# Four graph layers in one kernel: a longer lag between two streams of work, and plain f32 in place of split fp32r matmuls

## The chip, the cores and the metric

The kernel runs on one core of one Trainium2 chip. The metric is the time of one execution on the device in microseconds. The profile is one execution of the same program. In it PE is TensorE (PEld its weight loads), DVE is VectorE, ACT is ScalarE, POOL is GpSimd, and SP issues the transfers of inputs and outputs.

## What is computed

The input is 64 graphs of 256 nodes with 256 features, and a 0/1 adjacency matrix for each. Four layers follow each other; every one takes `h = relu(layernorm(x))` and adds its result to `x`.

```
# layer 0: attention with 4 heads of 64
Wh = h @ W;  e = leaky_relu(e_src[i] + e_dst[j], 0.2), masked by adj
x += elu(softmax(e) @ Wh)
# layer 1: attention with 4 heads and 5 edge types
w = sum over t of (adj == t+1) * (e_src[t, i] + e_dst[t, j])
w = leaky_relu(w, 0.01), masked where adj == 0
o = relu(softmax(w) @ Wh + bias) + Wh
x += layernorm(o, per head) * gamma + beta
# layer 2: attention with one head of 256
x += softmax(masked leaky_relu(src[i] + dst[j], 0.2)) @ Wh
# layer 3: three rounds of a gated graph unit on h
for i in range(3):
    aggr = A.T @ (h @ weight[i])        # A = (adj != 0)
    h = gru_cell(aggr, h, w_ih, w_hh, b_ih, b_hh)
x += h
```

## The kernel before

Two graphs are handled together, so there are NP = 32 pairs. A pair is 512 rows, in C = 4 blocks of 128 partitions. Two Python generators write out the work of a pair. `attention(xt, at)` (line 320) writes layers 0, 1 and 2; `gru(p, xt, at)` (line 438) writes layer 3. Each `yield` ends a step: attention has NA = 50 steps and the GRU NB = 32 (lines 538 and 539).

`together` (line 526) interleaves the steps of attention of pair p with those of the GRU of pair p - 1, in the proportion NA to NB, and it ends only when both are done (lines 541 to 548). So there are 33 slots: one with attention alone, 31 with both, one with the GRU alone. `load(p + 1)` is written at the start of slot p. Tiles come from pools with a fixed number of buffers: `loads` 3, `work` 2 unless said otherwise, `small` 3, and two pools of 4 PSUM banks each, `psa` for attention (and for the norm of the GRU) and `psb` for the rest of the GRU. The order of issue on each engine is made from the written order by a scheduler; it may move an instruction ahead of others when its operands and a buffer are there. Each engine then works through its own queue.

The steps of attention, as far as they matter here:

- `norm_t` (line 188) takes statistics of a row on DVE (193, 194), makes the inverse deviation on POOL (196, 197), normalises on DVE (200), transposes on PE (208) and applies the relu on ACT (211). For the GRU it also returns the rows themselves.
- `project` (line 228) multiplies by the layer's weights (233); ACT brings the result to SBUF (237).
- A head of layer 0 makes its scores (258, then 340 on DVE with the mask `cap0`), then `softmax_t` (275 and 277 on DVE, 280 on ACT, transposes 290 on PE, copies 297 on DVE and 299 on ACT), then `attend_head` (305 on PE, 314 on DVE).
- A head of layer 1 does five score broadcasts (258), one for each edge type. ACT adds the source score while it brings one to SBUF (377), and DVE copies it under the mask of that type (381). Softmax and attend follow as in layer 0.
- The end of layer 1 is a normalisation per head, on DVE, POOL and ACT in turn (387 to 407). Layer 2 has one head (267, 418, 432).

The broadcast of a row of destination scores to all partitions is a matmul. `dst_rows` (line 240) makes all rows of a layer by one accumulated matmul in f32 (244) and splits them into a high half in type fp32r (249) and the remainder (250), which lie on two groups of 32 partitions. `dst_row` (line 255) then multiplies them by a 0/1 column of `sel` in one fp32r matmul, whose sum over partitions puts the two halves together.

A round of the GRU aggregates over the graph (451), applies twelve gates, each a matmul group of 512 columns (467), with ACT, DVE and POOL work between them (478 to 495), and transposes the new state back to rows (508). The adjacency `am` (441) is 0/1. It is held in fp32r, and the rows are split into `hh` and `hl` (215 and 216 for the first round, 520 and 521 for the others), so the aggregation takes four fp32r matmuls where two f32 ones would be written. In the last round the rows are added to `x` (514, tile `y`, in the buffers of `xn`) and sent out (523).

Of the kernel before, what the change touches and what calls it, by code (L numbers as in the profile page):

```python
# [8 lines left out]
F32 = mybir.dt.float32  # L9
I32 = mybir.dt.int32  # L10
U8 = mybir.dt.uint8
F32R = mybir.dt.float32r
AF = mybir.ActivationFunctionType
OP = mybir.AluOpType
# [9 lines left out]
def kernel(  # L24
# [24 lines left out]


    nc = tc.nc
    B, N, D = x.shape
    H, T, E = a1_src.shape
    L = w3t.shape[0]
    P = 128
    DC = D // P
    C = 2 * N // P
    S = 2 * N
# [14 lines left out]
    w2e = consts.tile([P, DC, D + 1], F32, name="w2e")  # L73

    Q = 32
    w0d = consts.tile([P, DC, 2 * Q], F32, name="w0d")
    w1d = consts.tile([P, DC, 2 * Q], F32, name="w1d")
    nc.vector.memset(w0d, 0.0)
    nc.vector.memset(w1d, 0.0)

    sel = consts.tile([2 * Q, Q], F32R, name="sel")
    nc.vector.tensor_add(sel, ident[: 2 * Q, :Q], ident[: 2 * Q, Q : 2 * Q])
    w2d = consts.tile([P, DC, 1], F32, name="w2d")
# [19 lines left out]
    with tc.tile_pool(name="setup", bufs=1) as sp, tc.tile_pool(  # L103
# [19 lines left out]
        for dc in range(DC):  # L123
            for s, (d0, d1, d2) in enumerate(
                (
                    (w0e[:, dc, D:], w1e[:, dc, D:], w2e[:, dc, D:]),
                    (w0d[:, dc, :H], w1d[:, dc, :HT], w2d[:, dc, :]),
                )
# [12 lines left out]
                nc.vector.tensor_reduce(d2, tmp.rearrange("p h e -> p (h e)"), AX.X, OP.add)  # L141

        for dc in range(DC):
            nc.vector.tensor_copy(w0d[:, dc, Q : Q + H], w0d[:, dc, :H])
            nc.vector.tensor_copy(w1d[:, dc, Q : Q + HT], w1d[:, dc, :HT])

# [20 lines left out]

    loads = ctx.enter_context(tc.tile_pool(name="loads", bufs=3))
    work = ctx.enter_context(tc.tile_pool(name="work", bufs=2))
# [8 lines left out]
    def bank(pool):  # L178
        return pool.tile([P, S], F32, name="bank_" + pool.name, tag="bank_" + pool.name)
# [8 lines left out]
    def norm_t(xt, want_rows=False):  # L188
# [23 lines left out]
        if not want_rows:  # L212
            return ht
        hh, hl = halves()
        nc.vector.tensor_scalar(hh, xn, 0.0, None, op0=OP.max)
        nc.vector.scalar_tensor_tensor(
            hl, xn, 0.0, hh.bitcast(F32), op0=OP.max, op1=OP.subtract
        )
        return ht, (hh, hl)

    def halves():

        return (
            work.tile([P, C, D], F32R, name="hh"),
            work.tile([P, C, D], F32R, name="hl"),
        )

    def project(ht, we, m):
# [9 lines left out]
        return wh  # L238

    def dst_rows(ht, wd):  # L240

        ps = bank(psa)
        for dc in range(DC):
            nc.tensor.matmul(  # L244
                ps[: 2 * Q, :], lhsT=wd[:, dc, :], rhs=ht[:, dc, :],
                start=(dc == 0), stop=(dc == DC - 1),
            )
        ed = work.tile([2 * Q, S], F32R, name="ed")
        nc.scalar.copy(ed, ps[: 2 * Q, :])
        nc.vector.tensor_tensor(  # L250
            ed[Q:, :], ps[Q : 2 * Q, :], ed[Q:, :].bitcast(F32), op=OP.subtract
        )
        return ed

    def dst_row(ed, r):

        ps = bank(psa)
        nc.tensor.matmul(  # L258
            ps, lhsT=sel[:, r : r + 1].to_broadcast([2 * Q, P]), rhs=ed, start=True, stop=True
        )  # L260
        return ps

# [57 lines left out]
    def attention(xt, at):  # L320
# [10 lines left out]
        wh = project(ht, w0e, D + H)  # L331
        ed = dst_rows(ht, w0d)
        yield
        o = work.tile([P, C, D], F32, name="o")
        for h in range(H):
            ps = dst_row(ed, h)
            u = work.tile([P, C, N], F32, name="u", bufs=3)
            for c in range(C):
                b = c // 2
                nc.vector.scalar_tensor_tensor(  # L340
                    u[:, c, :], ps[:, b * N : (b + 1) * N], wh[:, c, D + h : D + h + 1],
                    cap0[:, c, :], op0=OP.add, op1=OP.min,
                )
            yield
            pt, rs = softmax_t(u, 0.2)
            yield
            attend_head(o, pt, rs, wh, h)
            yield
# [15 lines left out]
        wh = project(ht, w1e, D + HT)  # L364
        ed = dst_rows(ht, w1d)
        yield
        o = work.tile([P, C, D], F32, name="o")
        for h in range(H):
            u = work.tile([P, C, N], F32, name="u", bufs=3)
            nc.gpsimd.tensor_copy(u, base)  # L370
            for t in range(T):
                r = t * H + h
                ps = dst_row(ed, r)
                e = work.tile([P, C, N], F32, name="e")
# [63 lines left out]
    def gru(p, xt, at):  # L438

        am = work.tile([P, C, N], F32R, name="am", bufs=1)  # L440
        nc.vector.tensor_scalar(am, at, 0.0, None, op0=OP.not_equal)
        ht, hn = norm_t(xt, want_rows=True)
        yield
        for i in range(L):
            ag = work.tile([P, DC, S], F32, name="ag")
            for dc in range(DC):
                ps = bank(psb)
                for b in range(2):
                    for k in range(4):
                        part, c = hn[k % 2], 2 * b + k // 2  # L450
                        nc.tensor.matmul(  # L451
                            ps[:, b * N : (b + 1) * N],
                            lhsT=part[:, c, dc * P : (dc + 1) * P],
                            rhs=am[:, c, :],
                            start=(k == 0), stop=(k == 3),
                        )
                nc.scalar.copy(ag[:, dc, :], ps)
# [40 lines left out]
            last = i == L - 1  # L498
            if last:
                y = work.tile([P, C, D], F32, name="y", tag="xn")  # L500
            else:
                hn = halves()
            for b in range(2):
                ps = bank(psb)
                for ic in range(2):
                    for dc in range(DC):
# [4 lines left out]
                            ident,  # L511
                        )
                if last:
                    nc.vector.tensor_add(
                        y[:, 2 * b : 2 * b + 2, :].rearrange("p c d -> p (c d)"),
                        xt[:, 2 * b : 2 * b + 2, :].rearrange("p c d -> p (c d)"), ps,
                    )
                else:
                    hh, hl = (v[:, 2 * b : 2 * b + 2, :].rearrange("p c d -> p (c d)") for v in hn)
                    nc.scalar.copy(hh, ps)  # L520
                    nc.vector.tensor_tensor(hl, ps, hh.bitcast(F32), op=OP.subtract)
            yield
        nc.sync.dma_start(out_v[:, p * C : (p + 1) * C, :], y)
        yield

    def together(a, na, b, nb):

        done_a = done_b = 0
        ended = object()
        while a is not None or b is not None:  # L530
            if b is None or (a is not None and done_a * nb <= done_b * na):
                a = None if next(a, ended) is ended else a
                done_a += 1
            else:
                b = None if next(b, ended) is ended else b
                done_b += 1

    NA = 2 + 3 * H + 1 + H * (T + 2) + 3 + 4
    NB = 2 + L * (2 + 4 * DC)
    tiles = {0: load(0)}  # L540
    for p in range(NP + 1):
        if p + 1 < NP:
            tiles[p + 1] = load(p + 1)
        together(
            attention(*tiles[p]) if p < NP else None, NA,
            gru(p - 1, *tiles[p - 1]) if p else None, NB,
        )
        tiles.pop(p - 1, None)

# [37 lines left out]
```

## Time and profile before

Every number is in microseconds unless it says otherwise.

| what | value |
|---|---|
| time, median of 3 runs | 6597.33 (6597.02 to 6597.98) |
| time of the profiled execution | 6597.33 |
| its span, first to last instruction | 6595.5 |
| mean granted clock of TensorE | 0.80 of full |
| PE busy | 4860.4 (74%), 17584 records |
| weight loads busy | 2973.5 (45%) |
| DVE busy | 3744.0 (57%) |
| ACT busy | 2796.1 (42%) |
| POOL busy | 1445.3 (22%) |
| gates, line 467, PE | 1208.9 + 1151.3 |
| score broadcasts, line 258, PE | 336.0, 768 records |
| aggregation, line 451, PE | 269.4 + 269.8, 1536 records |
| eviction of layer 1 scores, line 377, ACT | 969.7 |
| masked copies of layer 1, line 381, DVE | 853.1 |
| bytes moved | 59.05 MB, mean 9 GB/s |

A busy PE is not a PE at its peak, since matmuls are pipelined and their ends are modelled. The granted clock is the share of full speed that TensorE's clock had. The time of the profiled execution is 1.8 over the span: what lies around the span is small and fixed. Where a view gives an idle time and an arrow, the instruction after the arrow is the one that ended the wait.

### The profile page before, as it was taken

To read this page: it belongs to the slowest core of one execution; us is meant where nothing else is said; L and a number is where in the kernel's file an instruction comes from. 1 tells how busy PE (TensorE), PEld (TensorE's weight loads), DVE (VectorE), ACT (ScalarE), POOL (GpSimd) and SP (SyncE) were. 2 spreads that over 40 slices of the span, in tenths; PEclk is the share of its full clock that TensorE was granted. 3 is DMA by queue.
4 is the path that set the end of the run, shared out by engine and by line. 5 is a ranking of instruction groups with operands and counts; after the bars stand their busy time and mean duration, and the time that the engine had idled before them with its cause. 6 is when DMAs were issued, how large, how long until landed. Compare 5 with 4: busy or idle time off the path is not lost.

```text
span 6595.5 us, 52281 instructions
## 1 busy us (share of the span) xinstructions
PE 4860.4 (74%) x17584; PEld 2973.5 (45%) x17584; DVE 3744.0 (57%) x5955; ACT 2796.1 (42%) x7021; POOL 1445.3 (22%) x935
## 2 busy tenths in 40 slices
PE   4676877777877768777778777687777787776877
PEld 2444544444544444444445444444444454444443
DVE  4555655655555556555555556565555555565653
ACT  2344443444533444434445334444344443344442
POOL 1222122221222221222212222212222122222121
PEclk6777888777878778887778787788877787877888
DMA  1000000000000000000000000000000000000000
GB/s 55 0 10 10 4 10 7 10 10 4 10 7 10 10 10 4 10 7 10 10 4 10 7 10 10 10 4 10 7 10 10 4 10 7 10 10 7 0 4 7
DMA packets 55356, 59.05 MB, mean 9 GB/s; under 512 B 3120, under 2 KB 54192, under 8 KB 55088
## 3 DMA queue, kind: packets, MB, share of 16 engines
q1 hardware_dynamic: 54080, 53.88, 2.7%
q8 instruction: 139, 2.28, 0.1%
q10 hardware_dynamic: 1008, 1.84, 0.1%
q14 instruction: 129, 1.06, 0.1%
HBM read 38.93 MB, written 16.78 MB: 8 GB/s over the span
## 4 chain that ended last, share of the span: by engine, by line
PE 57%; DVE 17%; ACT 13%; POOL 9%; issue 4%; DMA 0%; DVEq 0%; ACTq 0%; SPq 0%; POOLq 0%
PE bank_psb L467 23%; PE bank_psa L305 10%; ACT e L377 9%; PE bank_psa L233 6%; PE bank_psb L451 4%; PE bank_psa L290 4%; PE bank_psa L258 3%; PE bank_psa L208 2%; DVE u L275 2%; PE bank_psa L244 2%; POOL var L402 1%; POOL en L351 1%; DVE nm L277 1%; POOL d L493 1%; POOL o L405 1%
## 5 line engine op out<-in xcount | busy, mean ns | idle before, releaser
L467 PE MATMUL bank_psb<-ht,whh 128*128 128x512 f32 x2304 | 1208.9, 637 | 0.0
L467 PE MATMUL bank_psb<-ag,wc 128*128 128x512 f32 x2304 | 1151.3, 604 | 0.0
L377 ACT ACTIVATE e<-bank_psa,wh 128x256 f32<-128x256 f32 x2560 | 969.7, 481 | 175.7 <-PE bank_psa L258 174.6
L493 POOL TENSOR_TENSOR d<-ht,n 128x512 f32<-128x512 f32 x192 | 273.1, 1422 | 3329.0 <-ACT n L487 3329.0
L381 DVE COPY_PREDICATED u<-masks,e 128x1024 f32<-128x1024 uint8 x640 | 853.1, 1333 | 255.1 <-ACT e L377 247.6
L208 PE MATMUL bank_psa<-ident,xn 128*128 128x128 f32 x1024 | 205.4, 352 | 909.4 <-DVE xn L200 889.9
L280 ACT ACTIVATE u<-u,nm 128x256 f32<-128x256 f32 x1152 | 571.1, 497 | 619.0 <-DVE nm L277 619.0
L305 PEld LDWEIGHTS bank_psa<-wh,pt 128*128 128x128 f32 x4608 | 738.9, 233 | 124.4 <-issue 61.0
L305 PE MATMUL bank_psa<-wh,pt 128*128 128x64 f32 (+1 forms) x4608 | 788.8, 332 | 1.8
L290 PE MATMUL bank_psa<-ident,u 128*128 128x128 f32 x2304 | 480.3, 333 | 375.5 <-ACT u L280 373.8
L467 PEld LDWEIGHTS bank_psb<-ht,whh 128*128 128x128 f32 x2304 | 445.7, 206 | 445.6 <-issue 433.3
L290 PEld LDWEIGHTS bank_psa<-ident,u 128*128 128x128 f32 x2304 | 334.0, 167 | 677.8 <-ACT u L280 580.9
L208 PEld LDWEIGHTS bank_psa<-ident,xn 128*128 128x128 f32 x1024 | 155.2, 177 | 1018.2 <-issue 857.1
L467 PEld LDWEIGHTS bank_psb<-ag,wc 128*128 128x128 f32 x2304 | 402.4, 191 | 405.6 <-issue 405.0
L211 ACT ACTIVATE ht<-bank_psa 128x512 f32<-128x512 f32 x256 | 142.6, 595 | 942.5 <-PE bank_psa L208 939.0
L314 DVE TENSOR_TENSOR o<-bank_psa,rs 128x256 f32<-128x256 f32 x256 | 108.3, 423 | 535.8 <-PE bank_psa L305 535.8
L297 DVE COPY pt<-bank_psa 128x512 f32<-128x512 f32 x288 | 197.9, 687 | 330.6 <-PE bank_psa L290 326.3
L451 PE MATMUL bank_psb<-am,hh 128*128 128x256 f32 x768 | 269.4, 379 | 154.4 <-ACT hh L520 153.3
L508 PE MATMUL bank_psb<-ident,ht 128*128 128x128 f32 x768 | 195.7, 388 | 232.1 <-DVE ht L495 212.6
L275 DVE SCALAR_TENSOR_TENSOR u<-u 128x1024 f32<-128x1024 f32 x288 | 351.1, 1219 | 3.5
L277 DVE TENSOR_REDUCE nm<-u 128x4 f32<-128x1024 f32 x288 | 349.6, 1214 | 3.5
L258 PE MATMUL bank_psa<-ed,sel 64*128 64x512 f32 x768 | 336.0, 509 | 5.0 <-DVE ed L250 2.8
(98 smaller groups left out, 6541.7 us busy)
## 6 DMA issues: line engine op xcount, KB each, us to landing
xt<-in_x_dram SPq DMA_DIRECT2D x32, 512.0 KB, 4.7
at<-in_adj_dram SPq DMA_DIRECT2D x32, 512.0 KB, 3.8
out_dram<-y SPq DMA_DIRECT2D x32, 512.0 KB, 3.2
whh<-in_L_gnn_w_hh_dram SPq DMA_DIRECT2D x1, 768.0 KB, 10.1
w<-in_L_gnn_weight_dram SPq DMA_DIRECT2D x3, 256.0 KB, 3.0
wih<-in_L_gnn_w_ih_dram SPq DMA_DIRECT2D x1, 768.0 KB, 5.9
a1b<-in_L_gnn_a_src_dram ACTq DMA_DIRECT2D x1, 640.0 KB, 7.2
a1b<-in_L_gnn_a_dst_dram ACTq DMA_DIRECT2D x1, 640.0 KB, 10.2
```

Source lines behind the costliest of these rows:

```text
L208: nc.tensor.transpose(ps[:, c * P : (c + 1) * P], xn[:, c, dc * P : (dc + 1) * P], ident)
L233: nc.tensor.matmul(ps[:, :m], lhsT=ht[:, dc, c * P : (c + 1) * P], rhs=we[:, dc, :m], start=(dc == 0), stop=(dc == DC - 1),)
L258: nc.tensor.matmul(ps, lhsT=sel[:, r : r + 1].to_broadcast([2 * Q, P]), rhs=ed, start=True, stop=True)
L275: nc.vector.scalar_tensor_tensor(u, u, slope, u, op0=OP.mult, op1=OP.max)
L277: nc.vector.tensor_reduce(nm, u, AX.X, OP.max, negate=True)
L280: nc.scalar.activation(u[:, c, :], u[:, c, :], AF.Exp, bias=nm[:, c : c + 1], accum_out=sm[:, c : c + 1])
L290: nc.tensor.transpose(ps[:, jc * N + ic * P : jc * N + (ic + 1) * P], u[:, 2 * b + ic, jc * P : (jc + 1) * P], ident,)
L305: nc.tensor.matmul(ps, lhsT=pt[:, b, jc, ic * P : (ic + 1) * P], rhs=wh[:, 2 * b + jc, f0:f1], start=(jc == 0), stop=(jc == 1),)
L377: nc.scalar.activation(e[:, c, :], ps[:, b * N : (b + 1) * N], AF.Identity, bias=wh[:, c, D + r : D + r + 1],)
L381: nc.vector.copy_predicated(u, masks[:, t], e)
L451: nc.tensor.matmul(ps[:, b * N : (b + 1) * N], lhsT=part[:, c, dc * P : (dc + 1) * P], rhs=am[:, c, :], start=(k == 0), stop=(k == 3),)
L467: nc.tensor.matmul(ps, lhsT=w[:, dc, g * P : (g + 1) * P], rhs=v[:, dc, :], start=(k == 0), stop=(k == n - 1),)
```

## The change

Two things are changed together.

The first is the type of the matmuls with a 0/1 operand. All are plain f32 now. In layer 0 `dst_rows` is gone: each head computes and broadcasts its scores in one step with `dst_scores`, a function that layer 2 already used, with two accumulated matmuls of full depth. In layer 1 the rows are still made once (without the padding to 64) and copied once by ACT; each broadcast is one f32 matmul with a column of `ident`. In the GRU, `am` and the rows `hn` are f32, the aggregation takes two f32 matmuls instead of four fp32r ones, the relu of the first rows is one POOL instruction, and the later rows are brought back by one copy on DVE and one on ACT.

The second is the order of writing. The loop of slots is gone. One generator runs the attention of all pairs, another the GRU of all pairs. The GRU starts one and a half passes of attention later (`lag = NA + NA // 2`), and both then advance in the proportion NA to NB without a stop at the end of a pair. `loads` has four buffers in place of three, and the last rows take a buffer of `hn` in place of one of `xn`.

```diff
-    loads = ctx.enter_context(tc.tile_pool(name="loads", bufs=3))
+    loads = ctx.enter_context(tc.tile_pool(name="loads", bufs=4))
...
-        hh, hl = halves()
-        nc.vector.tensor_scalar(hh, xn, 0.0, None, op0=OP.max)
-        nc.vector.scalar_tensor_tensor(
-            hl, xn, 0.0, hh.bitcast(F32), op0=OP.max, op1=OP.subtract
-        )
-        return ht, (hh, hl)
+        hn = work.tile([P, C, D], F32, name="hn")
+        nc.gpsimd.tensor_scalar(hn, xn, 0.0, None, op0=OP.max)
+        return ht, hn
...
         ht = norm_t(xt)
         wh = project(ht, w0e, D + H)
-        ed = dst_rows(ht, w0d)
         yield
...
-            ps = dst_row(ed, h)
+            ps = dst_scores(ht, w0d, h)
...
-        ed = dst_rows(ht, w1d)
+        ps = bank(psa)
+        for dc in range(DC):
+            nc.tensor.matmul(
+                ps[:HT, :], lhsT=w1d[:, dc, :], rhs=ht[:, dc, :],
+                start=(dc == 0), stop=(dc == DC - 1),
+            )
+        ed = work.tile([HT, S], F32, name="ed", bufs=1)
+        nc.scalar.copy(ed, ps[:HT, :])
...
-                ps = dst_row(ed, r)
+                ps = bank(psa)
+                nc.tensor.matmul(
+                    ps, lhsT=ident[:HT, r : r + 1].to_broadcast([HT, P]), rhs=ed,
+                    start=True, stop=True,
+                )
...
-        am = work.tile([P, C, N], F32R, name="am", bufs=1)
+        am = work.tile([P, C, N], F32, name="am", bufs=1)
...
-                    for k in range(4):
-                        part, c = hn[k % 2], 2 * b + k // 2
+                    for sc in range(2):
                         nc.tensor.matmul(
                             ps[:, b * N : (b + 1) * N],
-                            lhsT=part[:, c, dc * P : (dc + 1) * P],
-                            rhs=am[:, c, :],
-                            start=(k == 0), stop=(k == 3),
+                            lhsT=hn[:, 2 * b + sc, dc * P : (dc + 1) * P],
+                            rhs=am[:, 2 * b + sc, :],
+                            start=(sc == 0), stop=(sc == 1),
                         )
...
-            if last:
-                y = work.tile([P, C, D], F32, name="y", tag="xn")
-            else:
-                hn = halves()
+            hn = work.tile([P, C, D], F32, name="hn")
...
+                elif b == 0:
+                    nc.vector.tensor_copy(dst, ps)
                 else:
-                    hh, hl = (v[:, 2 * b : 2 * b + 2, :].rearrange("p c d -> p (c d)") for v in hn)
-                    nc.scalar.copy(hh, ps)
-                    nc.vector.tensor_tensor(hl, ps, hh.bitcast(F32), op=OP.subtract)
+                    nc.scalar.copy(dst, ps)
...
-    tiles = {0: load(0)}
-    for p in range(NP + 1):
-        if p + 1 < NP:
-            tiles[p + 1] = load(p + 1)
-        together(
-            attention(*tiles[p]) if p < NP else None, NA,
-            gru(p - 1, *tiles[p - 1]) if p else None, NB,
-        )
-        tiles.pop(p - 1, None)
+    tiles = {}
+
+    def attentions():
+        for p in range(NP):
+            if p not in tiles:
+                tiles[p] = load(p)
+            if p + 1 < NP:
+                tiles[p + 1] = load(p + 1)
+            yield from attention(*tiles[p])
+
+    def grus():
+        for p in range(NP):
+            yield from gru(p, *tiles.pop(p))
...
+    lag = NA + NA // 2
+    a, b = attentions(), grus()
+    for k in range(NA * NP + lag):
+        next(a, None)
+        if k >= lag:
+            for _ in range((k - lag + 1) * NB // NA - (k - lag) * NB // NA):
+                next(b, None)
+    for _ in b:
+        pass
```

## The prediction

> **What bounds the kernel now.** I first asked how regular the run is. Line 388 runs once per pair; the answer for that line gives its first and last start, and so does that of line 208 for the first transposes of pair 0 and of the last GRU.
>
> ```profile
> L388 DVE SCALAR_TENSOR_TENSOR o<-o,wh x32: 1224/1226/1227, 216.7 to 6459.8; 128x1024 f32<-128x1024 f32 x32
> L208 PE MATMUL bank_psa<-ident,xn x1024: 272/328/477, 59.8 to 6507.7; 128*128 128x128 f32 x171
> ```
>
> (6459.8 - 216.7) / 31 = 201.4 us per pair. The span is 59.8 (set-up and first load) + 32 x 201.4 + about 92 for the last pair's GRU alone (its inputs are final at 6503, the span ends at 6595.5): 6596. So the question is the 201.4.
>
> I cut one steady pair at three marks: A, layer 0 (from the end of one attention to line 354), B, layer 1 up to line 388, C, the normalisation of layer 1 and layer 2. Below it are the same stretches of pair 0, where no GRU runs. Columns: length, then busy time of PE, PEld, DVE, ACT, POOL, then the granted clock.
>
> ```profile
> core 0: us, PE busy (x) PEld busy (x) DVE busy (x) ACT busy (x) POOL busy (x), PEclk, DMA share, GB/s
> 665.40:722.80 57.40, 55.31 (x232) 33.61 (x231) 33.30 (x55) 24.76 (x60) 9.47 (x7) 0.94 0.00 0
> 722.80:822.40 99.60, 76.31 (x253) 44.40 (x251) 61.13 (x79) 54.84 (x141) 14.15 (x9) 0.80 0.02 6
> 822.40:865.00 42.60, 17.51 (x60) 12.71 (x60) 20.89 (x49) 6.85 (x17) 20.85 (x12) 0.62 0.08 25
> ...
> 60.00:123.00 63.00, 35.71 (x128) 26.50 (x127) 25.15 (x42) 14.97 (x44) 7.17 (x5) 0.55 0.03 9
> 123.00:218.00 95.00, 42.14 (x144) 30.00 (x144) 49.67 (x61) 44.20 (x123) 8.29 (x5) 0.55 0.00 0
> 218.00:260.00 42.00, 17.04 (x55) 12.39 (x56) 18.88 (x44) 6.41 (x16) 20.86 (x12) 0.61 0.00 0
> ```
>
> The reader should see two things. A pair takes 200 us with or without its GRU: attention is a chain that no engine fills. And the GRU is not free: alone the chain runs at half clock, with the GRU at 0.94, and what the clock gives, the GRU's matmuls take. A is full (55.3 of 57.4), C is empty, because the GRU ended in B. The list of waits has that hole, and the chain of waits has the GRU's matmuls (467) ahead of attention's work:
>
> ```profile
> PE bank_psa L208 <- DVE xn L200: 889.9, 66, 24.4
> ...
> PE bank_psb L467 23%; PE bank_psa L305 10%; ACT e L377 9%; PE bank_psa L233 6%; PE bank_psb L451 4%; PE bank_psa L290 4%; PE bank_psa L258 3%; PE bank_psa L208 2%; DVE u L275 2%; PE bank_psa L244 2%; POOL var L402 1%; POOL en L351 1%; DVE nm L277 1%; POOL d L493 1%; POOL o L405 1%
> ```
>
> Next, what keeps the order. This is the timeline of pair 0 at the change from one head to the next:
>
> ```profile
> 79.17 3.68 PE L305 MATMUL bank_psa<-wh,pt 128*128 128x64 f32 x16
> ...
> 82.77 0.79 PE L258 MATMUL bank_psa<-ed,sel 64*128 64x512 f32 x1
> 82.88 0.42 DVE L314 TENSOR_TENSOR o<-bank_psa,rs 128x256 f32<-128x256 f32 x1 [3.69 <-PE bank_psa L305]
> 83.60 1.66 DVE L340 SCALAR_TENSOR_TENSOR u<-bank_psa,wh,cap 128x256 f32<-128x256 f32 x4 [0.30 <-PE bank_psa L258]
> ```
>
> The score of the next head needs only ed, ready 11 us before, and PE was idle in between; still it comes after line 305. Work that takes banks of pool psa keeps the written order. Other work doesn't: line 441, written for a GRU of the next slot, runs at 61.4. GRU matmuls take banks of psb and run ahead of their written place, but its norm_t takes psa.
>
> **What the Trainium skill says.** "TensorE: Matmul & The Clock Gate", Part 1, gives 1.2 GHz after an idle window of about 3.4 us and 2.4 GHz after a busy one; the trace agrees (0.50 where PE idles in C, 1.00 in dense GRU work). The same page, "Architectural detail", has ACT and DVE as strict FIFO and PE pulling only weight loads ahead; the matmuls of this trace agree, and so a score behind a GRU group waits for it. No page prices the fp32r type; the trace does.
>
> **The price of a matmul**, at clock 1.00, from the starts in the timeline:
>
> ```profile
> 384.45 1.88 PE L467 MATMUL bank_psb<-ht,whh 128*128 128x512 f32 x4
> 386.16 1.88 PE L467 MATMUL bank_psb<-ag,wc 128*128 128x512 f32 x4
> ...
> 380.26 0.72 PE L258 MATMUL bank_psa<-ed,sel 64*128 64x512 f32 x2
> ...
> 671.66 0.28 PE L451 MATMUL bank_psb<-am,hh 128*128 128x256 f32 x1
> 671.78 0.28 PE L451 MATMUL bank_psb<-am,hl 128*128 128x256 f32 x1
> ```
>
> An f32 matmul appears as two records: four records in 1.71, so 0.43 each and 0.86 for one matmul of 512 columns. The fp32r score is one record: two in 0.72 against 0.50 for one alone, so 0.22. The aggregation's records of 256 columns start 0.12 apart; in f32 I take half of 0.43, 0.215.
>
> **The change part by part**, per pair.
>
> PE work. Layer 1 scores: 20 x (0.86 - 0.22) = +12.8. Layer 0 scores, now two full-depth f32 matmuls per head: 4 x (1.72 - 0.22) = +6.0; its dst_rows goes: -1.7. Aggregation: 16 f32 records in place of 16 fp32r in each of 3 GRU layers: 48 x (0.215 - 0.12) = +4.6. Sum +21.7 us on 149 busy, 694 us over the run. What reaches the chain:
>
> Stage A. For heads 1 to 3 the score stands between line 305 and line 340: 1.5 later, less the 0.2 by which line 314 covers it: +3.9. Head 0 loses the cast and subtraction of ed: in the steady pair line 244 ends at 669.5 and line 340 starts at 671.55; -2. Net +2. At half clock a score costs 3.4 in place of 0.8 (+2.6 each, +6 net); if PE warms up during it, +2.
>
> Stage B. The first score of each head is exposed: 4 x 0.64 = 2.6; less line 250 (0.7): +1.9. The other 16 scores run under ACT's four evictions (969.7 us / 640 = 1.5 per score). In the half with GRU work, some 10 scores take 6.4 us of PE that is 80% busy: I charge half, +3. In the half without it, at half clock, a score lasts 1.7, over the 1.5 of ACT: +2. Sum +7; bounds +2 (all hidden) and +15 (all of the 12.8 and the 2).
>
> GRU. Aggregation +4.6, half charged: +2. Off DVE: lines 250 (1.4), 215 and 216 (1.9) and four of 0.68 for line 521, against two copies of 0.69: -4.6; off ACT two copies of 0.6 and a cast; half of it lay on the chain of GRU or attention at most: I take -1. POOL gains one relu over 1024 elements, 2.8 as on line 351; POOL is 22% busy, so it delays only the first aggregation of a pair, while attention runs: 0; uncovered, 2.8.
>
> The new order. GRU's norm_t uses psa, xn and the statistics tiles, so by the rule above it stands at its written place: one and a half passes after its attention began, inside head 1 of layer 1 of the next pair. From there it will run about 140 us as now (669 to 808): some 50 of B, all of C, some 45 of the next A. Then nothing is ready for it until the next midpoint. So the hole of PE moves from C to late A and early B, of some 60 us, rather than vanish. C: PE pieces at full clock (projection 5.5 to 3.8, transposes 2.1 to 1.0 and 2.4 to 1.0, line 305 5.1 to 3.5) save 5.7; against it stand five matmul groups of the chain, each behind half a GRU group on average (0.9), and GRU's lines 483, 486, 494, 495 (0.69 each) and 493 (1.3 on POOL, whose next chain operation then waits for ACT's line 487): about +6. Net 0. A and B lose a third of the GRU work: contention there is 57.4 against some 48 (63 alone, at full clock for its 35.7 of PE), and about 10 in B, so 20 x 1/3 = -7; and the 60 us of half clock cost +5 (63 alone against 57.4 in A is 5.6 for such a stretch). Net -2.
>
> Loads get a fourth buffer: at 9 GB/s mean and a load a pair ahead, 0. Its SP queue holds loads and outputs only.
>
> Sum: 2 + 7 + 2 - 1 + 0 - 2 = +8, less 2 because the norm_t of the GRU, now behind a started head, leaves the start of A: T = 201.4 + 6 = 207.5.
>
> Ends. Attention starts at 60 as before. When it ends, GRU 30, begun some 100 us earlier, has about 30 us left, and GRU 31 needs 92 + 3 for the f32 aggregation, 125 in all in place of 92. Time: 60 + 32 x 207.5 + 125 = 6825 us. The profiled execution took 6597.33, which is the median of the three runs, 1.8 over the span; I make no difference between the two.
>
> **The rivals.**
>
> 1. Faster. The GRU's matmuls spread evenly, PE stays warm throughout, and the relief outweighs the price: A falls to 50 + 2, B to 95 + 5, C to 42: T = 194, 60 + 6208 + 125 = 6393. For it: the chain has 27% GRU matmuls on it, and C's hole of 24 us is large. Against it: f32 hands back 21.7 of PE, and GRU work runs ahead of its written place whenever PE is free, so it bunches. It decides below T = (6595 - 185) / 32 = 200.3: the half pair of longer lag at the end costs 33 us, so a pair must gain 1.1 us before anything is won.
>
> 2. Slower by much: the GRU's waits enter the chain of C. POOL, DVE and ACT serve seven dependent steps there, and each queue holds them behind GRU instructions that wait for each other; at 1.5 us more for each of ten crossings C gets 15 longer, and with B's upper bound, A's +6: T = 216 to 220, up to 7200. For it: in the steady pair PE sits idle at 749 to 754 behind line 508.
>
> 3. No difference: T = 199.9 to 200.7.
>
> 4. The change doesn't do what it says, the order of issue still running the GRU as early as now. Then C stays empty and A and B pay all the f32: T near 217, about 7130. The pool order speaks against it; I count it with rival 2.
>
> **How the numbers follow.** Likeliest, T from 203 to 213 (6680 to 7000): 0.52. Rival 1 with its neighbours: 0.19. Rivals 2 and 4: 0.24. Same within 0.2%, which is about what a measurement of this kernel can tell from no change: 0.05. Slower 0.76. The range of 6480 to 7080 leaves out the better half of rival 1 and the worse part of rival 2, about 0.2.
>
> **What would show it.** Right: line 388 recurs every 207 us; C has PE busy above 30 us; line 208's wait of 889.9 is mostly gone; PE clock of late A near 0.6; no GRU matmul in some 60 us before its norm_t; PE busy up by 600 or more; the last GRU work begins about 125 before the end. Wrong: A under 53, or a clock above 0.9 in all stages (rival 1); C above 52 (rival 2); PE idle in C (rival 4). The least certain term is how much of the GRU's work delays attention.

## The result, and the profile after

The changed kernel takes 6754.74 us (median of 4, 6748.02 to 6759.49), the kernel before 6597.18 on the same chip. The ratio is 1.0238, 95% interval 1.022 to 1.0256: slower. 6825 was predicted, with a range of 6480 to 7080. The profiled execution took 6748.02, 1.8 over its span.

The lines have moved. Line 388 of before is now 354, 208 is 197, 467 is 432, 258 is 336 in layer 1 and 223 in layers 0 and 2, 377 is 343, 381 is 347, 432 is 398, 451 is 416, and 493, 494 and 495 are 458, 459 and 460.

The answers for two lines, with the first and the last start of each:

```profile
L354 DVE SCALAR_TENSOR_TENSOR o<-o,wh x32: 1224/1226/1227, 228.3 to 6583.7; 128x1024 f32<-128x1024 f32 x32
L197 PE MATMUL bank_psa<-ident,xn x1024: 272/421/478, 59.7 to 6653.8; 128*128 128x128 f32 x171
```

A pair takes (6583.7 - 228.3) / 31 = 205.0 in place of 201.4. This time from one pair to the next is called the period below. The 150.7 by which the span grew divides into 11.6 before the first of these marks (228.3 against 216.7), 31 x 3.62 = 112.3 between them, and 26.8 after the last (162.5 against 135.7).

A steady pair, cut at the same marks into A, B and C. Columns: length, busy time of PE, PEld, DVE, ACT and POOL, then the granted clock:

```profile
core 0: us, PE busy (x) PEld busy (x) DVE busy (x) ACT busy (x) POOL busy (x), PEclk, DMA share, GB/s
3150.30:3206.60 56.30, 48.00 (x205) 29.25 (x203) 31.86 (x51) 19.86 (x52) 8.86 (x6) 0.97 0.10 28
3206.60:3308.10 101.50, 88.87 (x261) 49.87 (x262) 57.27 (x79) 52.82 (x137) 15.27 (x10) 0.76 0.00 0
3308.10:3355.20 47.10, 35.50 (x114) 20.04 (x113) 25.51 (x49) 13.18 (x27) 23.98 (x14) 0.93 0.00 1
```

With its marks set as exactly, the kernel before has A 60.6, B 98.3, C 42.5 (the prediction's A of 57.4 began 1.8 late and ended 1.5 early, which adds 1.5 to its B). C is full of GRU work now, and warm, which means that PE's clock is granted near full (0.93; cold is half clock), and it is 4.6 longer. A is shorter by 4.3, B longer by 3.2. The sum of PE is 172.4; before it was 150.6 in these marks.

The list of waits and the chain of waits:

```profile
DVE u L347 <- ACT e L343: 634.8, 573, 12.0
PE bank_psa L197 <- DVE xn L189: 634.0, 66, 24.2
ACT e L343 <- PE bank_psa L336: 425.4, 252, 5.0
```

```profile
PE bank_psb L432 15%; PE bank_psa L336 11%; PE bank_psa L261 8%; PE bank_psa L212 6%; PE bank_psa L246 5%; PE bank_psa L223 4%; ACT e L343 4%; PE bank_psb L416 3%; DVE nm L233 2%; DVE u L347 2%; POOL cap L281 2%; ACT u L236 2%; PE bank_psa L197 2%; DVE u L295 2%; DVE st L182 1%
```

The scores of layer 1 hold up their eviction on ACT now (425.4, before 174.6), and through it the masked copies on DVE (634.8, before 247.6). The score broadcasts were 3% of the chain; they are 11% in layer 1, and line 223 in layers 0 and 2 has 4%. The gates fell from 23% to 15%.

Where the scores hurt is seen in the timeline of PE at the start of B:

```profile
3210.65 2.10 PE L197 MATMUL bank_psa<-ident,xn 128*128 128x128 f32 x8 [9.95 <-DVE xn L189]
3212.80 6.03 PE L212 MATMUL bank_psa<-w1e,ht 128*128 128x276 f32 x16
...
3240.68 8.90 PE L336 MATMUL bank_psa<-ed,ident 20*128 20x512 f32 x10
...
3251.73 3.35 PE L432 MATMUL bank_psb<-ht,whh 128*128 128x512 f32 x4 [0.25 <-ACT ht L200]
```

The last gate before this ran at 3195.0, so for 56 us no gate runs. PE is cold (clock 0.65 from 3206.6 to 3251.7), and the five scores of head 1 take 8.90 us in ten records: 1.78 each at half clock, over the 1.5 in which ACT brings one to SBUF. This is the half-clock part of the prediction's stage B, in the place where the hole was expected to end.

### The profile page after: what moved, and what is told of

Same layout as the page of the kernel before. It is cut to its first block, busy times and chain, and to the rows that moved or that the text cites. A ratio compares the mean times of both kernels' runs of the same rounds, so it can differ in the third digit from the quotient of the medians.

```text
span 6746.2 us, 53824 instructions
## 1 busy us (share of the span) xinstructions
PE 5576.1 (83%) x18480; PEld 3207.4 (48%) x18480; DVE 3687.4 (55%) x5756; ACT 2757.7 (41%) x6925; POOL 1537.6 (23%) x967
## 4 chain that ended last, share of the span: by engine, by line
PE 55%; DVE 20%; POOL 13%; ACT 8%; issue 3%; DMA 0%; DVEq 0%; SPq 0%; ACTq 0%; POOLq 0%
PE bank_psb L432 15%; PE bank_psa L336 11%; PE bank_psa L261 8%; PE bank_psa L212 6%; PE bank_psa L246 5%; PE bank_psa L223 4%; ACT e L343 4%; PE bank_psb L416 3%; DVE nm L233 2%; DVE u L347 2%; POOL cap L281 2%; ACT u L236 2%; PE bank_psa L197 2%; DVE u L295 2%; DVE st L182 1%
## 5 line engine op out<-in xcount | busy, mean ns | idle before, releaser
L432 PE MATMUL bank_psb<-ag,wc 128*128 128x512 f32 x2304 | 1212.1, 646 | 0.0
L347 DVE COPY_PREDICATED u<-masks,e 128x1024 f32<-128x1024 uint8 x640 | 861.9, 1347 | 635.5 <-ACT e L343 634.8
L343 ACT ACTIVATE e<-bank_psa,wh 128x256 f32<-128x256 f32 x2560 | 993.8, 479 | 442.0 <-PE bank_psa L336 425.4
L432 PE MATMUL bank_psb<-ht,whh 128*128 128x512 f32 x2304 | 1160.8, 617 | 7.7 <-ACT ht L200 7.7
L336 PE MATMUL bank_psa<-ed,ident 20*128 20x512 f32 x1280 | 780.0, 747 | 0.7 <-ACT ed L327 0.7
L197 PE MATMUL bank_psa<-ident,xn 128*128 128x128 f32 x1024 | 237.0, 396 | 634.0 <-DVE xn L189 634.0
L261 PE MATMUL bank_psa<-wh,pt 128*128 128x64 f32 (+1 forms) x4608 | 751.1, 322 | 0.2
L432 PEld LDWEIGHTS bank_psb<-ag,wc 128*128 128x128 f32 x2304 | 465.8, 209 | 581.1 <-issue 581.1
L416 PE MATMUL bank_psb<-am,hn 128*128 128x256 f32 x1536 | 455.7, 454 | 55.1 <-DVE hn L481 55.1
L336 PEld LDWEIGHTS bank_psa<-ed,ident 20*128 20x128 f32 x1280 | 265.1, 222 | 361.3 <-issue 266.8
L416 PEld LDWEIGHTS bank_psb<-am,hn 128*128 128x128 f32 x1536 | 337.4, 229 | 166.0 <-DVE hn L481 62.9
L332 POOL COPY u<-base 128x1024 f32<-128x1024 f32 x128 | 147.7, 1154 | 1046.0 <-PE bank_psa L246 1046.0
L253 DVE COPY pt<-bank_psa 128x512 f32<-128x512 f32 x288 | 199.0, 691 | 314.7 <-PE bank_psa L246 314.2
```

Of the source, the lines that this page charges most:

```text
L197: nc.tensor.transpose(ps[:, c * P : (c + 1) * P], xn[:, c, dc * P : (dc + 1) * P], ident)
L261: nc.tensor.matmul(ps, lhsT=pt[:, b, jc, ic * P : (ic + 1) * P], rhs=wh[:, 2 * b + jc, f0:f1], start=(jc == 0), stop=(jc == 1),)
L336: nc.tensor.matmul(ps, lhsT=ident[:HT, r : r + 1].to_broadcast([HT, P]), rhs=ed, start=True, stop=True,)
L343: nc.scalar.activation(e[:, c, :], ps[:, b * N : (b + 1) * N], AF.Identity, bias=wh[:, c, D + r : D + r + 1],)
L347: nc.vector.copy_predicated(u, masks[:, t], e)
L416: nc.tensor.matmul(ps[:, b * N : (b + 1) * N], lhsT=hn[:, 2 * b + sc, dc * P : (dc + 1) * P], rhs=am[:, 2 * b + sc, :], start=(sc == 0), s ...
```

## Which part costs what: eight corners

Scores, aggregation and order can each be had alone. Six further kernels, with before and after, make all eight combinations. "Split" is the fp32r form in two halves. The kernel before ran again beside each of these kernels and took 6600 to 6601; the ratios are to that. The stage lengths given for each kernel are means over pairs 2 to 30.

"Aggregation" stands for all that came with it: the matmuls, the relu, the copies of the later rows and their buffers. The order alone keeps three load buffers, the other kernels in the new order have four. That doesn't enter: in all eight every load after the first landed over 130 us before attention read it.

**The changed kernel with the scores in fp32r again.**

```diff
-            ps = dst_scores(ht, w0d, h)
+            ps = dst_row(ed, h)
...
-                ps = bank(psa)
-                nc.tensor.matmul(
-                    ps, lhsT=ident[:HT, r : r + 1].to_broadcast([HT, P]), rhs=ed,
-                    start=True, stop=True,
-                )
+                ps = dst_row(ed, r)
```

> The changed kernel with the scores of layers 0 and 1 back in fp32r, the aggregation in f32. Theory: the scores carry most of the price, 7 to 10 us per pair: 6435 to 6530. Rival: scores run under ACT's evictions and cost nothing: 6730 to 6760.

Measured: 6525.96 us (6524.8 to 6529.32), ratio to before 0.9888 (0.9873 to 0.9902): faster than both kernels, and in the range of its theory. The period is 198.1 (A 55.3, B 95.7, C 47.1), and 5.8 of the 6.9 that a pair gains lie in B.

**The changed kernel with the aggregation in fp32r halves again** (and `y` in a buffer of `xn`, as before).

```diff
-        hn = work.tile([P, C, D], F32, name="hn")
-        nc.gpsimd.tensor_scalar(hn, xn, 0.0, None, op0=OP.max)
-        return ht, hn
+        hh, hl = halves()
+        nc.vector.tensor_scalar(hh, xn, 0.0, None, op0=OP.max)
+        nc.vector.scalar_tensor_tensor(hl, xn, 0.0, hh.bitcast(F32), op0=OP.max, op1=OP.subtract)
+        return ht, (hh, hl)
```

> The changed kernel with the aggregation of the GRU back in fp32r halves (with their extra DVE and ACT work), the scores in f32. Theory: 4.6 us of PE work per pair, some of it exposed, less the DVE work that returns: 0 to 2 us per pair, 6690 to 6755. Rival: the aggregation is the price: below 6600.

Measured: 6970.48 us (6969.75 to 6971.27), ratio 1.056 (1.0545 to 1.0576). The period is 212.1 (58.1, 102.0, 52.0). Both expected ranges lie below it: plain f32 in the aggregation, more PE work, is a gain of 7 us per pair.

**The new order alone,** with the mathematics of before and three load buffers.

```diff
-    tiles = {0: load(0)}
-    for p in range(NP + 1):
...
+    lag = NA + NA // 2
+    a, b = attentions(), grus()
+    for k in range(NA * NP + lag):
...
```

> The new written order with the old fp32r matmuls (and three load buffers as before). Theory: the price of f32 is about 10 us per pair on the chain and the order gives some 6 us back per pair, so the period falls from 205.0 to about 195 and the time to 60 + 32 x 195 + 115 = 6415 (6370 to 6490), faster than both kernels. Rival: the order itself costs (a longer end, the GRU's instructions in stage C) and f32 is hidden: 6620 to 6720.

Measured: 6720.3 us (6719.26 to 6722.72), ratio 1.0182 (1.0167 to 1.0197), period 204.5 (57.3, 95.4, 52.1). The order by itself is a loss, as the rival had it; that f32 was hidden, which the rival also said, the other corners deny.

**Plain f32 alone,** in the old order: the changed kernel with `together`, its loop of slots and three load buffers put back.

> The f32 matmuls with the old slots and a lag of one pair. Theory: stage A is full of PE work in that order, so nearly all of the added PE work that falls there is paid; 10 to 13 us per pair, 6920 to 7010. Rival (f32 hidden, order costs): 6600 to 6650.

Measured: 6806.7 us (6785.84 to 6808.29), ratio 1.0302 (1.0284 to 1.0319), period 207.4 (57.1, 107.4, 43.0). It lies between the two expected ranges.

**The aggregation alone in f32,** in the old order: of the change only the lines on `am`, `hn` and the aggregation.

> The old order and the scores as before, with the aggregation alone in plain float32. In the new order float32 aggregation was worth 6.8 us per pair against the halves (211.6 to 205.0). Theory P: 4 to 5 of these belong to the place that the GRU's instructions took there, so in the old order it is worth little: period 200 to 202, 6560 to 6620 us. Theory Q: the halves cost 5 us or more in any order, so their removal brings the period to 195 to 197, 6390 to 6460 us. My prediction had it 2 us per pair dearer: 6660 us.

Measured: 6395.21 us (6394.47 to 6396.1), ratio 0.9689 (0.9674 to 0.9703), period 194.6 (57.7, 93.8, 43.0). The second theory, Q, was right in this run: the halves cost as much without the new order.

**The scores alone in f32,** in the old order.

> The old order and the aggregation in halves as before, with the scores alone in plain float32. My prediction sized this at 2 us in stage A and 7 in B: 6885 us. With float32 aggregation, in the old order, the same edit cost 411 us (6395 to 6807). If the edits add: 6990 to 7030 us. If the score matmuls are dear only beside float32 aggregation: 6830 to 6900 us.

Measured: 6896.17 us (6893.11 to 6898.5), ratio 1.0447 (1.0432 to 1.0463), period 210.5 (58.7, 109.7, 42.2). The prediction's own size was 6885. The edits don't add: with f32 aggregation the same scores cost 411.

All eight, median us:

| scores | aggregation | old order | new order | the order costs |
|---|---|---|---|---|
| split | split | 6601 (before) | 6720 | +119 |
| split | f32 | 6395 | 6526 | +131 |
| f32 | split | 6896 | 6970 | +74 |
| f32 | f32 | 6807 | 6755 (the change) | -52 |

So f32 scores cost 295 or 411 in the old order and 250 or 229 in the new; f32 aggregation gains 206 or 90 in the old and 194 or 216 in the new. Where it gains them differs. In the old order it takes 3.0 off A and 4.4 off B, and C grows by 0.5; in the new order it takes 1.9 off A and 5.0 off C, and B stays (+0.3). The order pays only in the one corner where both are f32. The change is a dear part, a cheap part and an order that is worth little, and the parts don't add up to better than 120 us.

## Why the order is worth so little: places in a queue

In the order alone, C takes 52.1. Its timeline near the end of C:

```profile
3322.80 2.79 POOL L326 TENSOR_SCALAR cap<-cap 128x1024 f32<-128x1024 f32 x1
3325.56 1.26 POOL L493 TENSOR_TENSOR d<-ht,n 128x512 f32<-128x512 f32 x1
...
3326.85 1.51 DVE L494 SCALAR_TENSOR_TENSOR d<-z,d 128x512 f32<-128x512 f32 x1 [4.42 <-POOL d L493]
...
3329.01 0.68 DVE L297 COPY pt<-bank_psa 128x512 f32<-128x512 f32 x1
```

The GRU's subtraction on POOL (493) stands behind two mask lines of the next pair (325, 326), each over 1024 elements. DVE waits 4.42 for it at line 494, and attention's copy (297), whose transposes were done at 3324.2, stands behind. This is what is meant by a place in a queue: a ready instruction of one stream behind a waiting one of the other. The next two runs move nothing but the lag, by one step and by three, which gives these instructions other places.

```diff
-    lag = NA + NA // 2
+    lag = NA + 24
```

> The order alone (0/1 operands in halves as before), with the GRU 24 steps of attention further behind than one pair instead of 25. In the order alone, with 25, stage C takes 52.1 us, and 4.4 us of it is vector engine work of attention (the copy of the transposed weights, L297) standing behind two instructions of the GRU (L494, L495) that wait for a subtraction on GpSimd, itself behind the cap lines of the next pair. With 24 the subtraction comes before the cap lines and L494 and L495 are not in C. Theory P (places in the queues): C 47 to 48.5, period 200 to 201.5, 6560 to 6620 us. Theory Q (the halves themselves cost this in the new order, wherever the GRU stands): C 51 to 53, period 204 to 206, 6690 to 6750 us.

Measured: 6555.35 us (6553.74 to 6556.05), ratio 0.9931 (0.9916 to 0.9946), period 199.1 (59.5, 95.5, 44.1). One step of fifty, 4 us of lag, is worth 165 us, more than the whole change under study. C lost 8.0, and A grew by 2.2. Lines 494 and 495 have left the end of C, and the copy (297) waits for nothing but its transposes. The wait at line 494 accounts for 4.4 of the 8.0; the rest was not isolated.

With `lag = NA + 28`:

> The order alone with 28 steps instead of 25. On GpSimd the subtraction now stands behind all three cap lines, later than before; on the vector engine the copy L297 stands ahead of L494 and L495. Theory P, with the vector engine's queue as the place: the same gain of 4 to 4.5 us in C, period 200 to 201.5, 6570 to 6630 us. If the wait on GpSimd itself were the price, C would be as long or longer: 52 to 56, 6720 to 6850 us. Theory Q: 6690 to 6750 us.

Measured: 6732.71 us (6731.93 to 6733.35), ratio 1.02 (1.0183 to 1.0217), period 204.7 (59.4, 98.2, 47.2). C fell by 4.9, as theory P, that of places, said; but A grew by 2.1 and B by 2.8, and the period is that of the order alone. The time is outside the range of theory P and inside that of Q. Theory P explains C. It doesn't tell what the instructions that left C do elsewhere: that has to be looked up in each order. Which instruction of A and B cost these 4.9 was not isolated.

The changed kernel has the same knot at another place. The timeline of its C:

```profile
3323.03 1.26 POOL L458 TENSOR_TENSOR d<-ht,n 128x512 f32<-128x512 f32 x1
3323.11 2.27 DVE L373 TENSOR_TENSOR xt<-xt,o 128x1024 f32<-128x1024 f32 x1 [3.88 <-POOL o L372]
...
3347.09 3.62 PE L261 MATMUL bank_psa<-wh,pt 128*128 128x256 f32 x16
3348.12 2.78 POOL L283 TENSOR_SCALAR cap<-cap 128x1024 f32<-128x1024 f32 x1
3350.86 1.27 POOL L458 TENSOR_TENSOR d<-ht,n 128x512 f32<-128x512 f32 x1
3352.16 0.69 DVE L459 SCALAR_TENSOR_TENSOR d<-z,d 128x512 f32<-128x512 f32 x1 [5.39 <-POOL d L458]
...
3353.50 1.65 DVE L398 SCALAR_TENSOR_TENSOR xt<-bank_psa,rs,xt 128x256 f32<-128x256 f32 x4
```

Here the copy of the weights is ahead, and it is attention's last update (398) that stands behind lines 459 and 460. It starts 6.4 after line 261 did. In the old order with f32 aggregation, where no GRU runs in C, it is 3.4, with PE at half clock:

```profile
3369.83 5.11 PE L295 MATMUL bank_psa<-wh,pt 128*128 128x256 f32 x16
...
3373.25 0.88 DVE L422 SCALAR_TENSOR_TENSOR xt<-bank_psa,rs,xt 128x256 f32<-128x256 f32 x2 [3.39 <-PE bank_psa L295]
```

So some 3.0 us of every pair are lost there, at the hand-over to the next pair. "TensorE: Matmul & The Clock Gate", section "Architectural detail", in the Trainium skill calls the queues of ACT and DVE strict FIFO, and these waits agree: 5.39 us at line 459, with a ready instruction behind it.

**How far behind the GRU may start.** The kernel with fp32r scores, with 12 steps in place of 25:

> The changed kernel with the scores in halves as before, with the GRU 12 steps further behind than one pair instead of 25. The end after the last attention work (118.7 us with 25) is shorter by about half of the difference to the 92 us of the kernel before, 12 us. If the period does not mind where the GRU's own start falls (198.0 with 25): 6505 to 6520 us. If the GRU's normalisation then stands across C and A instead of B, and its waits fall where attention has least cover: period 201 to 206, 6600 to 6760 us.

Measured: 6540.34 us (6534.24 to 6547.14), ratio 0.9909 (0.9894 to 0.9923). The end after the last update of attention is 98.9 in place of 118.2, a gain of 19. The period is 199.0 in place of 198.1 (A 61.1, B 92.7, C 45.4), and 31 x 0.86 = 27 takes more than that back. The time lies between the two expected ranges. With half the extra lag the kernel is 14 us slower, 0.2%.

## What C could gain from the clock

The kernel with f32 aggregation in the old order, with TensorE work in C that uses no other engine:

```diff
+        ps = bank(psb)
+        for k in range(48):
+            nc.tensor.matmul(ps, lhsT=ident, rhs=whh[:, 0, :S], start=True, stop=True)
         ht = norm_t(xt)
         wh = project(ht, w2e, D + 1)
```

> The old order with float32 aggregation (43.0 us for stage C at a granted clock of 0.62, period 194.5, 6395 us), plus 48 float32 matmuls of 512 columns per pair ahead of layer 2's normalisation, whose results nothing reads: TensorE work in C that uses no other engine. In the changed order the same pieces of attention's own TensorE work in C (L208, the projection, the transposes, the attend matmuls) took 4.9 us less at full clock, yet C was 4 us longer than here. If the clock is worth that much and the rest was the price of the GRU's instructions on the other engines: C 38 to 39.5, period 189.5 to 191.5, 6240 to 6300 us. If these pieces are not on the path, or the clock falls again before they run: C 42 to 44, 6380 to 6420 us. If the useless matmuls are still running when the normalisation is ready: C over 45, over 6450 us.

Measured: 6650.64 us (6648.02 to 6651.98), ratio 1.0074 (1.0058 to 1.0091), C 52.5, the third case expected: the useless matmuls were still running. They were sized wrongly. An f32 matmul is two records, and most of the 48 ran as one block of 36.27 us, longer than the 20 in which the normalisation gets ready. The timeline of PE in its C:

```profile
3249.45 36.27 PE L403 MATMUL bank_psb<-whh,ident 128*128 128x512 f32 x84
...
3297.94 2.38 PE L280 MATMUL bank_psa<-ident,u 128*128 128x128 f32 x8 [4.98 <-ACT u L270]
3300.11 4.59 PE L295 MATMUL bank_psa<-wh,pt 128*128 128x256 f32 x16
```

As a test of the clock's worth in C it is inconclusive in its time. It shows one thing: PE is cold again at line 280 (2.38, the half-clock price) after 4.98 idle, in keeping with the idle window of about 3.4 us that "TensorE: Matmul & The Clock Gate" in the Trainium skill gives in Part 1, on the clock gate. To keep C warm one would need work in that gap too.

## Where the halves were dear

The page's waits of the kernel before have a line that the prediction did not look at, and its timeline in B shows what it is:

```profile
PE bank_psb L451 <- ACT hh L520: 153.3, 32, 5.2
```

```profile
3178.47 7.56 ACT L377 ACTIVATE e<-bank_psa,wh 128x256 f32<-128x256 f32 x20 [3.50 <-PE bank_psa L258]
...
3185.90 1.09 ACT L520 CAST hh<-bank_psb 128x512 fp32r<-128x512 f32 x2
...
3186.56 0.80 PE L451 MATMUL bank_psb<-am,hh 128*128 128x256 f32 x2 [4.92 <-ACT hh L520]
...
3193.87 0.60 PE L290 MATMUL bank_psa<-ident,u 128*128 128x128 f32 x4
```

Once per pair the GRU's cast (520) stands on ACT behind twenty evictions of attention's scores, PE waits 4.9 for it, cools, and then runs the whole aggregation as one block at half clock (3186.56 to 3191.2) before attention's transposes. To see whether it is this or the five vector instructions for the halves, the next kernel keeps those instructions and makes the matmuls f32. (As in the change, the last rows take a buffer of `hn`.)

```diff
+        nc.vector.tensor_scalar(hn, xn, 0.0, None, op0=OP.max)
+        rest = work.tile([P, C, D], F32R, name="rest", bufs=1)
+        nc.vector.scalar_tensor_tensor(rest, xn, 0.0, hn, op0=OP.max, op1=OP.subtract)
...
+                    nc.scalar.copy(dst, ps)
+                    rest = work.tile([P, C, D], F32R, name="rest", bufs=1)
+                    nc.vector.tensor_tensor(
+                        rest[:, 2 * b : 2 * b + 2, :].rearrange("p c d -> p (c d)"), ps, dst, op=OP.subtract
+                    )
```

> The old order with the aggregation's matmuls in float32, but with the instructions of the halves kept on the vector and scalar engines: the relu, the two subtractions (into a tile that nothing reads) and both copies on the scalar engine, as before. Theory (the halves cost through their instructions in the vector engine's queue, 4.7 us per pair): most of the 202 us comes back, 6540 to 6620 us. Rival (the form of the matmuls, 32 short ones against 16, or that the second half comes late, is the cost): 6390 to 6440 us.

Measured: 6286.99 us (6285.26 to 6287.75), ratio 0.9524 (0.951 to 0.9539), period 191.1 (57.6, 91.0, 42.5). The theory of the vector instructions falls: with all of them in, it is 313 us faster than before. The time is also 103 us below the rival's range. Its timeline of PE at the same place:

```profile
3230.52 1.54 PE L496 MATMUL bank_psb<-ident,ht 128*128 128x128 f32 x6 [7.60 <-DVE ht L486]
3232.10 1.22 PE L442 MATMUL bank_psb<-am,hn 128*128 128x256 f32 x2
3233.11 1.27 PE L282 MATMUL bank_psa<-ident,u 128*128 128x128 f32 x5
```

The aggregation comes in pieces between attention's transposes, and it doesn't wait for the copy. But PE idles just ahead of it all the same, for 7.60, since the GRU's new state (486) comes late, and PE is as cold there (clock 0.52).

**The same without the useless subtractions** (five instructions per pair, 4.0 us of DVE in all):

> The previous kernel with the useless subtractions taken out: old order, scores in halves, aggregation in plain float32, the relu of the first rows on the vector engine and both copies of the later rows on the scalar engine. It has four vector engine instructions per pair more than two, 4.0 us, less than the previous one. If the vector engine's busy time is what matters, this is at least as fast: 6220 to 6287 us. If what matters is which instructions of the GRU come to stand ahead of attention's in the queues, which every edit shuffles, it lies anywhere between the two neighbours or past them: 6290 to 6400 us. In the profile the first theory needs the period under 191.1 us with stage B under 91.

Measured: 6285.26 us (6284.15 to 6286.19), ratio 0.9522 (0.9506 to 0.9538), period 191.1 (57.6, 91.0, 42.5). This is the best kernel found. The 4.0 us of vector work per pair were worth 1.7 us over the whole run: nothing. What sets it apart from the first kernel with f32 aggregation (6395) is the relu on DVE and both copies on ACT. These are worth 110 us, though in the 6395 kernel PE hardly waited for the relu on POOL (once, for 2.2 us) or for the copy on DVE (0.9 over the run). Place is the likely cause; which instruction it is was not isolated.

**Is the wait at line 451 what the halves cost?** The runs speak against it. In three of the four pairs of corners PE hardly has this wait: 4.2 us over the run with f32 scores in the old order, 0.7 and 0.3 in the two kernels of the new order. f32 aggregation still gains 90, 194 and 216 in them. (The weight loads ahead of these matmuls wait 45, 39 and 2 for the halves, against 220 in the kernel before.) With a lag of 24 steps PE waits 157 for `hh` and 49 for `hl`, and that kernel is fast. And the start of each attention instruction, counted from the end of the pair before, shows where the kernel before falls behind the one with f32 matmuls (means over pairs 2 to 30):

| attention has reached | behind by |
|---|---|
| the end of layer 0 (line 354) | 3.1 |
| the first masked copy of head 0 in layer 1 (381) | 5.9 |
| the first masked copy of head 1 | 8.2 |
| the softmax of head 1 (275), just before the block | 8.2 |
| the end of that head (314), after the block | 9.2 |
| the end of the pair | 10.3 |

The stretch with the wait and the block holds 1.0 of the 10.3. More is lost at the end of head 0. There the GRU has run out of gates in the kernel before, PE idles, and attention's own matmuls run at half clock:

```profile
3171.02 1.61 PE L290 MATMUL bank_psa<-ident,u 128*128 128x128 f32 x5 [4.62 <-ACT u L280]
...
3174.14 3.52 PE L305 MATMUL bank_psa<-wh,pt 128*128 128x64 f32 x16
```

In the f32 kernel gates fill the same place, and PE is at full clock:

```profile
3213.79 1.88 PE L458 MATMUL bank_psb<-ht,whh 128*128 128x512 f32 x4
...
3217.41 0.49 PE L282 MATMUL bank_psa<-ident,u 128*128 128x128 f32 x3
3217.73 1.00 PE L297 MATMUL bank_psa<-wh,pt 128*128 128x64 f32 x8
```

So shown is that the halves cost 90 to 316 us in the old order, that their vector instructions don't account for it, and that most of it lies away from the wait. It fits the theory of places: the form of the aggregation shifts where the GRU stands beside attention. What shifts it was not isolated, and an indirect effect of the wait is not excluded.

## Why the prediction was right, point by point

The sign, the rank of the cases and the time (6755 for 6825) hold. So do four of the signs named: the period (205.0 for 207), PE busy in C (35.5, over 30), PE busy over the run (+716, over 600) and 56 us without a gate (some 60). The parts hold less well. Taken in the prediction's order, scores, then aggregation, then order, the corners give these steps (in another sequence they are others, as the table of the eight shows):

| step of the prediction | predicted | measured |
|---|---|---|
| scores (A +2, B +7), 32 pairs | +288 | +295 (6601 to 6896) |
| GRU aggregation +2, DVE -1, 32 pairs | +32 | -90 (6896 to 6807) |
| new order (-2 -2) x 32, end +33 | -95 | -52 (6807 to 6755) |
| sum | +225 | +154 |

- **PE work:** +21.7 predicted, 172.4 - 150.6 = +21.8 in the steady pair.
- **Scores:** right in the new order, A +0.9 and B +5.8 for +2 and +7. In the old order, with the halves, the sum is right by luck: A fell by 1.9 and B grew by 11.5. That B pays, partly in a cold stretch where a score takes longer than ACT's eviction, is shown: 8.90 for five.
- **Aggregation, the step that failed:** "+4.6, half charged: +2". It has the wrong sign: the step gained 90, and from the kernel before it gains 206. The prediction charged only PE time for it. It did not ask what the form changes in the waits around it, or where it leaves the GRU beside attention; the cause of the gain stays open.
- **DVE -1:** in the old order 4.0 us of these vector instructions are worth nothing per pair. POOL's relu at 0 is right as to waits: PE doesn't wait for it in the changed kernel.
- **New order, stages:** with all in f32 it takes 0.8 off A and 5.9 off B and adds 4.1 to C. Predicted were -2 for A and B together, -2 at the start of A and 0 for C.
- **Stage C, net 0:** C +4.6 in all. Between the kernels with fp32r scores and f32 aggregation, the clock saves 15.1 - 11.1 = 4.0 on lines 208, 233, 290 and 305 (5.7 predicted), and C still grows from 43.0 to 47.1, so crossings cost 8 (6 predicted). Some 3.0 of it is the last update behind line 459. The changed kernel shows 1.5 more, line 448 between 231 and 233, and 1.0 at line 373, which takes 2.27 in place of 1.23. Rival 2's mechanism was there, at 8 of its 15 us.
- **Where the GRU runs:** half right. Its transposes (197) keep their written place, but its statistics, its rows and the first aggregation (416) run ahead at the start of B. The gates then wait for the transposes. Only the last 11 us of A lie in the stretch without gates (clock 0.85 there, 0.6 predicted); the cold part is B up to head 1 (0.65).
- **The wait for `xn`** fell from 889.9 to 634.0, not "mostly gone": the hole of 24 in C became one of about 10 at the start of B and one of 9 in C.
- **End:** 125 predicted from attention's last update, 118.2 measured.
- **Not foreseen:** 11.6 in the first pair, where no GRU warms PE and the f32 scores run at half clock. Set against B's cost it was small.

The errors partly cancelled: -122 from the aggregation, +43 from the order, +7 from the scores. That 6755 came so near 6825 is in part luck, and the mechanism was right for the scores, half right for the order and wrong for the aggregation.

## What to carry to other kernels

When two streams share in-order queues, the PE time of a matmul is a poor price for its form: here the cheaper form of the aggregation cost more in all four comparisons, and its longest wait explained little of it. Before you blame a wait, compare where the two kernels drift apart. Vary a lag or an order by a single step before you judge it, since one step moved this kernel by 165 us. And take a bundled change apart: the best kernel here, 6285 us, keeps only f32 in the aggregation, with the relu and the copies on other engines than in the change.

## What the runs showed of the hardware

The DVE instruction at line 373, with two inputs from SBUF of 1024 elements each, took 2.3 in 31 pairs of the changed kernel, each time beside the POOL instruction of line 458, and 1.2 in the one pair without it. In the kernel before (line 407) it took 1.2 in all 32, with no POOL instruction beside it. The skill's "GPSIMD Engine Reference", section "Specifications", has the two engines share SBUF interfaces, with contention for vector instructions of two SBUF inputs; the trace agrees. So the GRU's small subtraction on POOL, 1.26 long, also cost attention's instruction on DVE 1.0.
